# Two fused graph layers, 32 batches of 512 x 512: constant loads as steps, a vector fold in 32-column products, an earlier range check, and new step lists at both ends

## The chip, the cores and the metric

The kernel runs on one core of a Trainium2 chip, in float32 throughout. The metric is the device time of one execution in microseconds. The kernel before was timed three times: median 3287.41 us, from 3285.51 to 3288.52. PE is the engine of matrix products, DVE the vector engine, ACT the scalar engine, POOL the GpSimd engine. SP issues the transfers (DMAs) and computes nothing. Matrix products leave their sums in PSUM banks; all other tiles stand in SBUF.

## What is computed

For each of 32 batches there is a matrix x of 512 nodes by 512 features and a 512 x 512 adjacency, whose rows sum to one. Two layers follow one another:

```python
# layer 0: eight heads of width 64, attention weighted by the adjacency
q, k, v = heads(x @ Wq.T + bq), heads(x @ Wk.T + bk), heads(x @ Wv.T + bv)
logits = q @ k.T / sqrt(64) + log(clip(adj, 1e-8))
x = layer_norm(x + (softmax(logits) @ v) @ Wo.T + bo, gamma, beta)
# layer 1: one head, logits from two vectors, masked by the adjacency
f = x @ fc_w.T + fc_b
logits = (f @ q_w.T + q_b) + (f @ k_w.T + k_b).T + (1 - adj) * -1e9
x = softmax(leaky_relu(logits)) @ f + x
```

The exponential of the logarithm of the adjacency is the adjacency itself, so the kernel multiplies exp(q k) by max(adj, 1e-8) instead of adding a logarithm.

## The kernel before

**Staging.** All work of a batch b is cut into named steps, small functions that each issue a few instructions. A batch has two halves: `first_two` treats head pairs 0 and 1, `second_two` pairs 2 and 3. While batch b is in attention, the halves also carry the output product and layer norm of batch b−1 and layer 1 of batches b−1 and b−2, and the x products of batch b+1. The order of the instructions of PE, DVE, ACT and SP is written by hand: under `manual_schedule` each engine's program has the order in which `perform` calls the steps. There is a list of step names for each half: FIRST and SECOND for batches 2 to 30, and special ones for batch 0 (FIRST0, SECOND0), batch 1 (FIRST1, SECOND1) and batch 31 (FIRST_LAST, SECOND_LAST). Each engine works in order, so a step that waits holds all that stands behind it on its engine, and only on its engine. SP's transfers go round robin over eight semaphores, so that an issue waits until the transfer issued eight before it has landed.

**Steps by name.** S0 to S7 are scores of a head pair (PE, L919, K by Q, 64 rows deep) and their exponentials on ACT (L926 in halves, L928 whole). f.. multiplies by the adjacency (DVE, L934), V.. is the value product (PE, L991, 64 columns for each of two heads), s.. and t.. are sums over the keys (DVE, L946, L950, L957; PE, L1056). The large weight products use Strassen's scheme in Winograd's form: seven products of quarters (`seven`, L226, its matmuls at L221, 64 columns at a time) with additions on DVE and ACT around them. Prefixes name the product: v (values; step m7 of it is vm7, which leaves through the copy L786), p, q and Q (queries and keys of one pair, with the copies L723 and L731 on ACT and additions at L727 on DVE), w (output weights of layer 0), o and O (the last product of layer 1), z (its fc product). d0 to d3 are the differences of x that the v and q products use (DVE, L695). c0 to c3 transpose a quarter of the adjacency each (DVE, L667). g and h are the sums of quarters of the weights wv, wq and wk (DVE, L183, L194). W, O, x, L, H, J, Y, Z steps are the versions for the last batches.

**Head.** Ahead of all steps the load of x of batch 0, the two column blocks `pair`, the weights wv, wq, wk (`load_first_constants`, L159), the adjacency of batch 0 in sixteen pieces (`load_a`, issued at L604) and then the weights wo and fc with bo, gamma, beta and the biases (`load_constants`, L169) are issued on SP. `fold_steps` (L235) issues the loads of fc_b, q_w, k_w, bv and columns of gamma and beta when it is called, also ahead of all steps. X, E and A are the transposes of x of batch 0, their copies, and the first query and key.

**Fold.** Some vectors are folded into others once: bv·Wo into bo (B0, B1), beta·fc into the constant row cc (O0), the products of fc with q_w and k_w (D0 to D7, L265), gamma into fc (G0 to G3, DVE, L306), and the two result vectors spread over all partitions (P0, P1, L284 and L285) as uq and uk. B0 and O0 use `row_times` (L251): four matmuls of 128 x 128 against 128 x 512 in which each column of the vector is broadcast to 128 columns, so that the row that comes out stands in all partitions.

**Range check.** The kernel computes softmaxes without subtracting the maximum, and counts as it goes whether all sums are in range. Steps rg0, rg1, rg2 (`find_range`, L1145 to L1171) reduce these counts to one flag: DVE over the elements, a transpose on PE (`pf`), DVE, a second transpose (`pone`), DVE. In the list they stand at the end. Then every engine loads the flag and branches past a general version of the kernel, which is there for data out of range and does not run here.

**End.** In SECOND_LAST the last product of layer 1 comes in parts (m20, m21 are halves of m2), with additions (a.., b..) on DVE and stores t0 to t4 on SP. `ost0` and `ost1` store the two halves of batch 30's result.

The steps of the last product, among others, have this form:

```python
"rg0": over, "rg1": turn, "rg2": store_flag
...
"m20": lambda: mul(2, "b", ns=(0,)),
"b01": lambda: add_rows(0, 1, "c"), "t2": lambda: store(0, 2, 1),
```

Of the kernel before, what the change touches and what calls it, by code (L numbers as in the profile page):

```python
# [9 lines left out]
FP = mybir.dt.float32  # L10
I32 = mybir.dt.int32
AF = mybir.ActivationFunctionType
# [7 lines left out]
P = 128  # L20
# [5 lines left out]
BL = 32  # L26
# [4 lines left out]
def kernel(  # L31
# [55 lines left out]
    nc = tc.nc  # L87
    B, N, D = x.shape
    DK = D // HEADS
    NC = N // P  # L90
    DC = D // P
# [16 lines left out]
    seen = const.tile([P, 2 * B + 1], FP, name="seen")  # L108
    k_cols = const.tile([P, BL], FP, name="k_cols")
# [4 lines left out]
    def load_weight(w, name, pieces=1):  # L114
        w_sb = const.tile([P, DC, D], FP, name=name)
        load_b(w_sb, w, pieces)
        return w_sb

    def load_row(pool, v, name):
        v_sb = pool.tile([P, v.shape[0]], FP, name=name)  # L120
        nc.sync.dma_start(out=v_sb, in_=v.partition_broadcast(P))
        return v_sb
# [36 lines left out]
    def load_first_constants(pair):  # L159

        for dst, w in zip(pair, (wqT, wkT)):
            nc.sync.dma_start(out=dst, in_=w[:, :P].rearrange("(c p) d -> p c d", p=P))
        K["bq"] = load_col(const, bq, "bq")
        K["bk"] = load_col(const, bk, "bk")
        K["wv"] = load_weight(wvT, "wv")
        K["wq"] = load_weight(wqT, "wq")
        K["wk"] = load_weight(wkT, "wk")

    def load_constants():  # L169
        K["wo"] = load_weight(woT, "wo")  # L170
        K["fc"] = load_weight(fcT, "fc")
        K["bo"] = load_row(const, bo, "bo")
        K["gamma"] = load_row(const, gamma, "gamma")
        K["cc"] = load_row(const, beta, "cc")
        K["q0"] = load_row(const, q_b, "q0")
        K["k0"] = load_row(const, k_b, "k0")
        for name in ("uq", "uk"):
            K[name] = const.tile([P, D], FP, name=name)
        K["qk_s"] = const.tile([P, 3, KH, D], FP, name="qk_s")
        for name in ("v_s", "wo_s", "fc_s"):  # L180
            K[name] = const.tile([P, 3, KH, H], FP, name=name)

# [52 lines left out]
    def fold_steps(banks, psum_parts, scratch):  # L235
# [9 lines left out]
        for row, vec in ((fcb, fc_b), (qw, q_w), (kw, k_w)):  # L245
            nc.sync.dma_start(out=row, in_=vec.partition_broadcast(P))
        with nc.allow_non_contiguous_dma("three vectors"):
            for col, vec in ((bvc, bv), (gc, gamma), (bc, beta)):
                nc.sync.dma_start(out=col, in_=vec.rearrange("(c p) -> p c", p=P))

        def row_times(col, w, bank):  # L251
            for c in range(DC):
                nc.tensor.matmul(
                    bank, col[:, c : c + 1].to_broadcast([P, P]), w[:, c, :],
                    start=(c == 0), stop=(c == DC - 1),
                )
            return bank
# [9 lines left out]
        def constant():  # L267
            cc = K["cc"]
            nc.vector.tensor_add(cc, cc, row_times(bc, K["fc"], banks[1]))
            nc.vector.tensor_add(cc, cc, fcb)  # L270
            nc.vector.tensor_sub(cc[:, H:], cc[:, H:], cc[:, :H])
# [10 lines left out]
        def spread(vector, bank):  # L282
            _, _, _, dg, name, _ = vector
            nc.tensor.matmul(bank, ones, dg, start=True, stop=True)  # L284
            nc.vector.tensor_copy(K[name], bank)  # L285

        def last_parts():
# [9 lines left out]
            "B0": lambda: nc.vector.tensor_add(bo, bo, row_times(bvc, K["wo"], banks[0])),  # L297
# [6 lines left out]
            for i, v in enumerate(vectors) for c in range(DC)  # L304
        } | {
            f"G{c}": lambda c=c: nc.vector.tensor_scalar_mul(  # L306
                fc[:, c, :], fc[:, c, :], gc[:, c : c + 1])
            for c in range(DC)
        }
# [256 lines left out]
    def fast(ctx):  # L566
# [790 lines left out]
        def numbered(steps, prefix):  # L1357
            return {f"{prefix}{i}": step for i, step in enumerate(steps)}
# [134 lines left out]
        def end_steps(b, banks):  # L1493
# [74 lines left out]
            X0 X1 X2 X3 E1 E3 E0 d0 E2 d1 g0 A0 g3 A1 g1 h0 h1 h2 g4 vm1 vcb vm5 vm6  # L1568
            c0 h3 c2 vc12 vm2 d3 vm7 vc22 g2 d2 va22 vc11 c1 vm3 vm4 vc21 h4 va12 S0
            S1 S2 c3 S3 pm1 pcb D0 pm5 pm6 pck2 pm2 pcq2 pcq1 f02 D1 D2 pm4 pm3 pck1  # L1570
            pm7 paq2 pak1 D3 S4 S5 pak2 S6 f12 f10 f03 f01 S7 B0 qm1 qm5 qcb qm6 f00
            qm2 V0a D4 qck2 qcq2 qcq1 ldx f11 qm3 f13 qm7 D5 D6 qaq2 V0b Qm1 D7 V0e
            qak2 qm4 Qcb Qm6 Qm2 B1 s00 qck1 Qm5 s01 Qck2 Qcq2 Qcq1 s02 V1a t00 t01
            V1b s10 V1e s11 Qm7 Qak2 Qm4 Qm3 Qck1 Qak1 Qaq2 s12
        """
        SECOND0 = """
            S0 r0 x0 S1 S2 r3 S3 x1 f22 t10 S4 d0 t11 f21 S5 S6 f20 f23 x3 mv0 S7 x2
            d1 O0 f31 qm1 qm5 V2a dv0 V2b r1 vm1 qck2 qcb qm6 vcb qm2 vm2 d3 s20 f30
            qcq1 V2e qcq2 qm7 G3 G0 qm3 vc11 f32 V3a vm5 f33 d2 s21 s22 V3b vc22
            qak2 vm6 qm4 qaq2 Qm1 qck1 s30 Qcb Qm5 Qck2 vc12 O1 V3e O2 vm3 la Qm6  # L1580
            vm7 s31 s32 Qm2 Qm4 Qm3 c0 Qck1 sc01 va12 r2 va22 Qcq1 Qcq2 t20 vm4 G1
            c1 G2 Qaq2 Qm7 c2 Qak2 Qak1 vc21 c3 sc00
        """
        FIRST1 = """
            t30 S0 S1 t21 t31 S2 S3 f03 f00 f01 S4 S5 S6 f12 mv2 f10 f02 S7 P0 P1
            qm1 qm5 qcb dv2 qck2 qm6 V0a V0b V0e s00 qm2 f11 qm3 qcq1 s01 P2 qcq2
            qm7 f13 qak2 wseed wm1 V1a ldx V1b qaq2 qm4 ldn s02 qck1 wcb V1e fd Qm1
            sc20 sc21 Qm5 fs ws11 t00 s10 wm2 s11 wm6 wm5 ws12 Qck2 wa01 t01 wa11
            Qcb Qm6 wm7 wm3 wa00 wb11 wm4 Qm2 Qm4 s12 wb01 b0 wa10 Qm3 Qcq2 b1 Qcq1
            b2 Qm7 b3 Qck1 Qaq2 Qak1 Qak2  # L1590
        """
        SECOND1 = """
            x0 n0 le1 S0 S1 n2 S2 x2 x1 n4 t10 le0 S3 k1 t11 S4 mv0 S5 mk0 d0 n1 S6
            vm1 k3 n3 x3 S7 k0 qm1 vcb qm5 d1 qcb qck2 R0 k2 u1 k4 d3 kst mk1 f20
            f21 vm5 vm6 vc12 u3 V2a qm6 vc22 u0 f22 f23 u2 qm2 qcq1 qcq2 f30 qm7 u4
            kld f31 f32 V2b dv0 R1 d2 lg0 lg1 f33 V2e vm7 qm3 vm3 lk1 lg2 V3a qak2
            V3b qaq2 lg3 lk2 qm4 lk0 nm lk3 s20 ex2 va12 ex3 Qm1 qck1 R3 vm2 la R2
            ex0 ex1 inv s21 c0 s30 Qcb nr1 nr0 va22 nr3 vc11 s22 V3e Qm5 s31 nr2 Qm6
            Qck2 Qm2 Qcq1 Qm4 Qm3 Qcq2 vm4 t20 s32 c2 Qm7 Qak2 Qck1 sc01 Qak1 c1
            vc21 Qaq2 bl sc00 c3  # L1600
        """
        FIRST_LAST = """
            t21 S0 f00 S1 t30 f01 t31 mv2 S2 S3 y0 S4 f02 e0 S5 S6 e1 zs1 S7 V0a qm1
            qcb qm5 qm6 qm2 qck2 zm1 zcb qm3 y1 f03 qcq2 V0b zA21 zA11 e2 e3 zt1
            zE11 f11 qcq1 zm2 zm5 zm6 zA12 zE12 zc22 zc12 zm3 qaq2 zm7 dv2 Qm1 Qcb
            qm7 fd s00 za12 zE21 s01 za22 qak2 f10 Qm6 zm4 f13 V0e f12 ldn s02 zc21
            t00 Qm2 sc21 qm4 sc20 V1a V1b fs wseed s10 wm1 s11 ws11 s12 zc11 wcb wm5
            wm2 qck1 wa11 Qm5 Qcq2 ws12 wm6 wm3 wa00 wa01 wm7 Qck2 Qm4 wb01 Qcq1 b0
            wb11 wm4 t01 Qm3 b1 Qck1 wa10 Qm7 b2 b3 Qaq2 Qak2 V1e Qak1
        """  # L1610
        SECOND_LAST = """
            t10 n0 zd S0 S1 S2 S3 S4 S5 f20 f23 f21 S6 oseed t11 S7 f22 f31 V2a om1
            n1 zs f30 mv0 ldn H20 n2 V2b n4 k1 n3 k0 k3 k2 os11 H30 u0 ocb om2 k4 u2
            H21 V2e u1 kst f32 om5 om6 os12 u3 le0 u4 V3a dv0 oa00 oa01 H22 f33 om7
            H23 oa11 ob11 H31 kld H32 H24 mk0 V3b V3e H33 Wal sc00 om4 om3 sc01
            Wseed lg1 lk1 yn Wfs lg0 H34 Wm1 Wm5 Wfd lk0 Wcb le1 Ws11 Wa11 mk1 lg3
            lg2 Wm6 Wa01 Wm2 nm ex1 Ws12 lk3 ex0 ex3 Wm7 lk2 Wa00 Wb11 ex2 inv ob01
            nr3 oa10 Wm3 ost1 Wm4 Wb01 b0 nr1 Wa10 nr0 b1 b2 nr2 J0 J1 J2 b3 Lal xn0
            J3 y1 xn1 xk0 xn2 xn3 xle0 xn4 xk1 xk2 ost0 xk3 xk4 xkst Z0 Z1 xu0 y0
            xu2 Yd Z2 xmk0 LN2 xu1 xle1 xkld xmk1 Oseed Z3 Om1 xu3 xu4 Ys xlg1 Os11  # L1620
            xlg0 Ocb xlk1 xlg3 Om5 xlg2 Om6 Oa01 Oa11 Om2 xnm xlk0 Os12 Om7 xlk3
            xex1 xex0 xlk2 Ob11 xex3 xex2 xinv xnr0 Om3 xnr3 Om4 Ob01 LN0 LN1 Lp0
            xnr1 Oa10 Lp1 Ost1 xnr2 Lp2 Oa00 Ost0 Lp3 Le0 Le2 LN3 Le1 Lm1 LT0 Le3
            LT2 LT1 LT3 Lm5 Lcb Ly Lc22 Lm6 Lc12 Lm7 Lm2 La22 Lm4 Lm3 La12 LZ0 Lc11
            LZ1 Lc21 Loseed LZ3 Lom1 Lom4 Locb Lom21 Loa001 Lom20 LZ2 Lom6 Lom5
            Loa10 Loa01 Loa11 Lom7 Loa000 Lot3 Lob10 Lot4 Lob11 Lot0 Lot1 Lom3 Lob01
            rg0 rg1 Lot2 rg2
# [5 lines left out]
        load_a(0, range(NC))  # L1633
        load_constants()
# [9 lines left out]
        head |= fold  # L1644
# [151 lines left out]
```

## Time and profile before

| quantity | value |
|---|---|
| median of three runs | 3287.41 us |
| profiled execution | 3286.61 us |
| its span on the core | 3282.6 us |
| PE busy | 3258.3 us (99%) |
| DVE busy | 3080.4 us (94%) |
| ACT busy | 1471.5 us (45%) |
| POOL busy | 1.0 us |
| mean granted clock of PE | 0.998 |
| HBM read, written | 184.00 MB, 36.72 MB |
| factor products (L934), 512 | 608.7 us, 1210 ns each |
| fold products (L253), 16 records | 592 ns each by the median |

The span is what the profiler sees of the program, the time of the execution is a little longer on both sides. "Busy" is the time in which an engine executes; PE at 99% leaves little idle time for the whole program, and the profile's view of waits lists which engine waited for what, and how long. The chain that ended last follows the work back from the last instruction, and shows which instruction each step had to wait for. A table of stretches gives for each part of the span the busy time of each engine and, as PEclk, the share of PE's full clock that was granted. Batch 2 begins its scores at 198.8 us and batch 31 at 3119.8 us, so a batch takes about 101 us: (3119.8 − 198.8) / 29. The lists that the change lays anew run before the first of these times and after the second.

### The profile page before, as it was taken

To read this page: it belongs to the slowest core of one execution; us is meant where nothing else is said; L and a number is where in the kernel's file an instruction comes from. 1 tells how busy PE (TensorE), PEld (TensorE's weight loads), DVE (VectorE), ACT (ScalarE), POOL (GpSimd) and SP (SyncE) were. 2 spreads that over 40 slices of the span, in tenths; PEclk is the share of its full clock that TensorE was granted. 3 is DMA by queue.
4 is the path that set the end of the run, shared out by engine and by line. 5 is a ranking of instruction groups with operands and counts; after the bars stand their busy time and mean duration, and the time that the engine had idled before them with its cause. 6 is when DMAs were issued, how large, how long until landed. Compare 5 with 4: busy or idle time off the path is not lost.

```text
span 3282.6 us, 64089 instructions
## 1 busy us (share of the span) xinstructions
PE 3258.3 (99%) x25586; PEld 1890.9 (58%) x25586; DVE 3080.4 (94%) x5329; ACT 1471.5 (45%) x2762; POOL 1.0 (0%) x10
## 2 busy tenths in 40 slices
PE   8999999999999999999999999999999999999998
PEld 4555555555655555555555555555555555555655
DVE  6999999999999999999999999999999999999997
ACT  3335534444444454444544444444435534444444
POOL 0000000000000000000000000000000000000000
PEclk9999999999999999999999999999999999999999
DMA  5343433433434434335343344343343443443322
GB/s 129 55 70 71 89 72 66 88 88 72 84 68 74 96 66 91 71 62 95 79 81 82 60 83 93 67 88 68 70 95 70 89 73 67 86 89 71 84 58 67
DMA packets 917263, 256.44 MB, mean 78 GB/s; under 512 B 842720, under 2 KB 844768, under 8 KB 916960
## 3 DMA queue, kind: packets, MB, share of 16 engines
q1 hardware_dynamic: 916960, 252.30, 38.6%
q8 instruction: 203, 3.33, 0.4%
q14 instruction: 100, 0.82, 0.1%
HBM read 184.00 MB, written 36.72 MB: 67 GB/s over the span
## 4 chain that ended last, share of the span: by engine, by line
PE 97%; SPq 1%; ACT 1%; DVE 1%; DMA 0%; issue 0%; DVEq 0%; ACTq 0%
PE f L221 23%; PE my L221 15%; PE mz L221 15%; PE mx L221 15%; PE po L991 13%; PE sc L919 6%; PE mx L919 2%; PE my L919 2%; PE mz L919 2%; SPq L604 0%; SPq L150 0%; PE mx L334 0%; ACT at L926 0%; PE ps L1056 0%; ACT at L928 0%
## 5 line engine op out<-in xcount | busy, mean ns | idle before, releaser
L934 DVE SCALAR_TENSOR_TENSOR at<-cT,at 128x1024 f32<-128x1024 f32 x512 | 608.7, 1210 | 3.3 <-ACT at L928 3.3
L991 PE MATMUL po<-at,v 128*64 128x512 f32 x2048 | 485.1, 595 | 0.1
L723 ACT ACTIVATE qT<-f,bq 128x256 f32<-128x256 f32 x254 | 115.8, 471 | 805.0 <-PE f L221 805.0
L946 DVE TENSOR_TENSOR at<-at,at 128x1024 f32<-128x1024 f32 x378 | 454.5, 1209 | 2.4 <-PE po L991 2.1
L991 PEld LDWEIGHTS po<-at,v 128*64 128x64 f32 x2048 | 141.6, 137 | 223.9 <-issue 131.9
L221 PE MATMUL f<-xT,wq 128*64 128x256 f32 x2032 | 262.7, 379 | 0.5 <-ACT at L928 0.5
L928 ACT ACTIVATE at<-sc 128x1024 f32<-128x1024 f32 x256 | 259.1, 1073 | 5.0 <-DVE ks L957 2.5
L221 PE MATMUL f<-T,qk_s 128*64 128x256 f32 x2032 | 257.0, 379 | 0.4 <-ACT at L928 0.3
L919 PE MATMUL sc<-qT,kT 64*128 64x512 f32 x1024 | 241.9, 589 | 0.0
L221 PEld LDWEIGHTS f<-xT,wq 128*64 128x64 f32 x2032 | 145.5, 137 | 103.0 <-issue 36.3
L221 PEld LDWEIGHTS f<-T,qk_s 128*64 128x64 f32 x2032 | 145.4, 137 | 87.7 <-issue 17.1
L723 ACT ACTIVATE kT<-f,bk 128x256 f32<-128x256 f32 x254 | 120.1, 473 | 136.9 <-PE f L221 128.8
L919 PEld LDWEIGHTS sc<-qT,kT 64*128 64x128 f32 x1024 | 100.4, 187 | 119.6 <-issue 74.9
L950 DVE STREAM_TRANSPOSE at<-at 128x1024 f32<-128x1024 f32 x126 | 154.5, 1226 | 1.1
L957 DVE TENSOR_REDUCE ks<-at 128x32 f32<-128x1024 f32 x126 | 151.5, 1203 | 1.0
L919 PE MATMUL so<-qT,kT 64*128 64x512 f32 x256 | 137.1, 615 | 0.0
L919 PE MATMUL mx<-qT,kT 64*128 64x512 f32 x256 | 132.7, 598 | 1.2 <-ACT v L786 0.7
L919 PE MATMUL mz<-qT,kT 64*128 64x512 f32 x256 | 132.6, 598 | 0.0
L919 PE MATMUL my<-qT,kT 64*128 64x512 f32 x256 | 132.4, 597 | 0.0
L221 PE MATMUL f<-xT,wk 128*64 128x256 f32 x1016 | 131.3, 379 | 1.0 <-ACT qT L723 1.0
L221 PE MATMUL f<-T,wk 128*64 128x256 f32 x1016 | 131.3, 379 | 0.9 <-ACT kT L723 0.9
L221 PE MATMUL f<-xT,qk_s 128*64 128x256 f32 x1016 | 131.2, 379 | 0.0
(383 smaller groups left out, 6380.9 us busy)
## 6 DMA issues: line engine op xcount, KB each, us to landing
cT<-in_adj_dram SPq DMA_DIRECT2D x512, 64.0 KB
R<-d SPq DMA_DIRECT2D x126, 256.0 KB
x<-in_x_dram SPq DMA_DIRECT2D x124, 256.0 KB
L<-in_adj_dram SPq DMA_DIRECT2D x62, 512.0 KB
n<-in_x_dram SPq DMA_DIRECT2D x31, 1024.0 KB
out_dram<-yb SPq DMA_DIRECT2D x62, 512.0 KB
eP<-L SPq DMA_DIRECT2D x480, 64.0 KB
w<-dk SPq DMA_DIRECT2D x32, 256.0 KB
```

The source lines that it names most:

```text
L221: nc.tensor.matmul(to[ts(h, DK)], left[:, ts(h, DK)], right, start=start, stop=stop, skip_group_check=True,)
L723: nc.scalar.activation(of(w, half), ps[bank], AF.Identity, bias=bias)
L919: nc.tensor.matmul(parts[j], s["kT", p][rows, ts(kc, P)], s["qT", p][rows, :], start=True, stop=True,)
L928: nc.scalar.activation(at, sc, AF.Exp, scale=SCALE)
L934: nc.vector.scalar_tensor_tensor(at, cT[:, kc, :].unsqueeze(1).to_broadcast([P, 2, N]), ADJ_MIN, at, ALU.max, ALU.mult,)
L946: nc.vector.tensor_add(to, to, s["at", p, kc])
L950: nc.vector.transpose(flat, flat)
L957: nc.vector.tensor_reduce(ks.rearrange("p h m -> p (h m)"), flat.rearrange("p (a k) -> p a k", k=BL), AX.X, ALU.add,)
L991: nc.tensor.matmul(s["po", p][j * DK : (j + 1) * DK, :], s["v"][h // 4][:, kc, ts(h % 4, DK)], s["at", p, kc][:, j, :], start=(kc == 0), s ...
```

## The change

It has four parts.

1. **Loads as steps.** The loads of wv, wq, wk, wo, fc, the row vectors, the columns and the first adjacency (now in four quarters, la0 to la3, of four pieces each) become steps of the list FIRST0. They stand at the places where the list has them, and SP issues them in that order: wv; quarter 1 of the adjacency; q_w; quarter 2; wk; fc; beta's row; bo; k_w; wo; gamma; wq; bv; quarters 3 and 0; q_b; fc_b; beta's column; k_b; gamma's column; then x of batch 1.
2. **The fold.** `row_times` is replaced by `quarter_rows` and `row_sum`. Each of the four matmuls broadcasts its column of the vector to 32 columns, and writes one quarter of the partitions of a bank, so the four sums stand side by side. ACT copies the bank to SBUF. One further product with `pick`, a column that is 1 at partitions 0, 32, 64 and 96 and else 0, broadcast to 128 columns, adds the four. There are two new steps, Bq and Oq, ahead of B0 and O0. G0 to G3 and the copies of P0 and P1 go from DVE to ACT. POOL gets five small memsets for `pick`.
3. **The range check** goes from the end of SECOND_LAST to places before the last products: rg0 among the O products, rg1 and rg2 among the last products of layer 1, so that pf, pone and the flag stand ahead of Lom3 and Lob11.
4. **The six special lists** are laid anew. In FIRST0, d3 stands ahead of all transposes of the adjacency. In SECOND1, n0 to n3 stand ahead of S0. In SECOND_LAST, the first half of the last product (Lom20), its addition (Loa000) and the stores Lot2 and Lot3 come last, and the store Ost0 of batch 30 after these.

The core of the diff, with the lists cut to the places that are spoken of:

```diff
+    pick = const.tile([P, 1], FP, name="pick")
+    nc.gpsimd.memset(pick, 0.0)
+    for i in range(P // BL):
+        nc.gpsimd.memset(pick[i * BL : i * BL + 1], 1.0)
...
-    def load_weight(w, name, pieces=1):
-        w_sb = const.tile([P, DC, D], FP, name=name)
-        load_b(w_sb, w, pieces)
-        return w_sb
+    def load_weight(w, name):
+        w_sb = K[name] = const.tile([P, DC, D], FP, name=name)
+        return lambda: load_b(w_sb, w)
...
-        def row_times(col, w, bank):
+        def quarter_rows(col, w, bank):
+
             for c in range(DC):
                 nc.tensor.matmul(
-                    bank, col[:, c : c + 1].to_broadcast([P, P]), w[:, c, :],
-                    start=(c == 0), stop=(c == DC - 1),
+                    bank[c * BL : (c + 1) * BL, :], col[:, c : c + 1].to_broadcast([P, BL]),
+                    w[:, c, :], start=True, stop=True,
                 )
+            nc.scalar.copy(more[:, 3, :], bank)
+
+        def row_sum(bank):
+            nc.tensor.matmul(
+                bank, pick.to_broadcast([P, P]), more[:, 3, :], start=True, stop=True)
             return bank
...
-            nc.vector.tensor_copy(K[name], bank)
+            nc.scalar.copy(K[name], bank)
...
-            "B0": lambda: nc.vector.tensor_add(bo, bo, row_times(bvc, K["wo"], banks[0])),
+            "Bq": lambda: quarter_rows(bvc, K["wo"], banks[0]),
+            "Oq": lambda: quarter_rows(bc, fc, banks[1]),
+            "B0": lambda: nc.vector.tensor_add(bo, bo, row_sum(banks[0])),
...
-            f"G{c}": lambda c=c: nc.vector.tensor_scalar_mul(
-                fc[:, c, :], fc[:, c, :], gc[:, c : c + 1])
+            f"G{c}": lambda c=c: nc.scalar.activation(
+                fc[:, c, :], fc[:, c, :], AF.Identity, scale=gc[:, c : c + 1])
...
         FIRST0 = """
-            X0 X1 X2 X3 E1 E3 E0 d0 E2 d1 g0 A0 g3 A1 g1 h0 h1 h2 g4 vm1 vcb vm5 vm6
-            c0 h3 c2 vc12 vm2 d3 vm7 vc22 g2 d2 va22 vc11 c1 vm3 vm4 vc21 h4 va12 S0
-            S1 S2 c3 S3 pm1 pcb D0 pm5 pm6 pck2 pm2 pcq2 pcq1 f02 D1 D2 pm4 pm3 pck1
-            pm7 paq2 pak1 D3 S4 S5 pak2 S6 f12 f10 f03 f01 S7 B0 qm1 qm5 qcb qm6 f00
...
+            X0 lwv X1 X2 la1 X3 E1 lf1 la2 E3 E0 d0 E2 A0 d1 g0 A1 d3 lwk lfc g1 g3
+            lcc vm1 vm5 g2 lbo vcb lf2 h0 lwo vm6 vc12 d2 vm2 lgamma vm7 vc22 g4 vm3
+            vc11 D0 va22 va12 vm4 vc21 h4 S0 S1 lwq S2 S3 lv0 h3 pm1 h1 pcb c2 pm5
+            pm6 pck2 pm2 h2 pm4 D1 pm3 la3 la0 c0 f00 D2 pcq1 pcq2 c3 pck1 paq2 pm7
+            pak1 lq0 S4 c1 S5 pak2 S6 S7 D3 f03 Bq f01 f10 qm1 f02 qcb qm5 V0a lf0
+            V0b qck2 lv2 f11 f13 V0e lk0 f12 qm6 qm2 D4 s00 s01 s02 B0 qcq2 qm3 qcq1
...
         SECOND0 = """
+            S0 S1 S2 t10 t11 x0 x1 x2 S3 d0 x3 d1 S4 f20 S5 f22 S6 S7 Oq qm1 G0 qcb
+            qm5 G2 f30 vm1 f31 mv0 f21 O0 qck2 f23 vcb d3 f33 f32 O1 la V2a dv0 c1
...
         SECOND1 = """
-            x0 n0 le1 S0 S1 n2 S2 x2 x1 n4 t10 le0 S3 k1 t11 S4 mv0 S5 mk0 d0 n1 S6
-            vm1 k3 n3 x3 S7 k0 qm1 vcb qm5 d1 qcb qck2 R0 k2 u1 k4 d3 kst mk1 f20
...
+            n0 t10 n1 n2 n3 S0 le0 k0 x0 t11 n4 x1 f20 S1 S2 S3 x3 le1 k1 x2 S4 S5
+            k2 S6 S7 k3 d0 vm1 mv0 k4 f23 qm1 kst kld qm5 vcb f21 d1 qcb qm6 u0 qck2
...
         SECOND_LAST = """
-            LZ1 Lc21 Loseed LZ3 Lom1 Lom4 Locb Lom21 Loa001 Lom20 LZ2 Lom6 Lom5
-            Loa10 Loa01 Loa11 Lom7 Loa000 Lot3 Lob10 Lot4 Lob11 Lot0 Lot1 Lom3 Lob01
-            rg0 rg1 Lot2 rg2
...
+            Ob01 Lp1 Lp2 rg0 Oa10 Lp3 LN2 LN1 LN3 Le0 Le1 LT0 Le2 Le3 Lm1 LT1 Lcb
+            Lm6 LT2 Lc12 Lm5 LT3 Lc22 Lm7 Lm2 Lc11 La22 Lm4 Ly Lc21 Lm3 La12 Loseed
+            Lom1 LZ0 Locb LZ1 Lom4 Loa10 Lom6 Lom21 LZ2 LZ3 Loa001 rg1 Loa01 Lom5
+            Loa11 Lom7 rg2 Ost1 Lom3 Lob11 Lot4 Lot0 Lob10 Lob01 Lot1 Lom20 Lot2
+            Loa000 Lot3 Ost0
...
         load_first_constants(pair)
-        load_a(0, range(NC))
-        load_constants()
+        loads = constant_steps() | numbered([lambda kc=kc: load_a(0, (kc,)) for kc in range(NC)], "la")
```

## The prediction

> **What bounds the kernel now.** The page of the profile comes first: its span, the busy shares, and the shares of the chain that ended last.
>
> ```profile
> span 3282.6 us, 64089 instructions
> ...
> PE 3258.3 (99%) x25586; PEld 1890.9 (58%) x25586; DVE 3080.4 (94%) x5329; ACT 1471.5 (45%) x2762; POOL 1.0 (0%) x10
> ...
> PE 97%; SPq 1%; ACT 1%; DVE 1%; DMA 0%; issue 0%; DVEq 0%; ACTq 0%
> ```
>
> PE is the bound: 3282.6 − 3258.3 leaves 24.3 us in which it is idle. Batches 2 to 30 keep their order, so the change can win only three things: idle time of PE at both ends, PE work at both ends, and half-speed stretches. The waits of PE say where the idle time is (us in total, times, longest).
>
> ```profile
> PE mx L221 <- DVE xT L695: 3.5, 1, 3.5
> PE my L221 <- ACT at L926: 2.2, 1, 2.2
> PE pf L1162 <- DVE low L1158: 1.9, 1, 1.9
> PE pw_a L221 <- DVE oT L846: 1.2, 1, 1.2
> ```
>
> 3.5 us are in batch 0's V product, 2.2 in SECOND1, 1.9 in the range check, 1.2 in SECOND_LAST. The chain that ended last, in order of time (start, us, what), tells what lies behind the first.
>
> ```profile
> 21.72 2.43 DMA cT<-in_adj_dram
> ...
> 24.28 0.71 DVE cT L667
> 24.99 0.59 DVE xT L695
> 25.58 0.14 issue
> 25.71 3.63 PE mx L221 x16
> 29.34 1.73 PE my L221 x16
> ...
> 48.22 3.63 PE mx L253 x8
> ```
>
> DVE works in order. The last x difference (d3, L695) stands behind the adjacency transposes c0 and c2 (L667), which wait for the transfer of the adjacency. PE stood from 22.18 to 25.71, and vm7 then took 3.63 us where its neighbour of the same size took 1.73. The table of stretches says why (us, PE busy, ..., PEclk, DMA share, GB/s).
>
> ```profile
> 22.00:26.00 4.00, 0.52 (x6) 0.30 (x4) 3.43 (x5) 0.59 (x1) 0.00 (x0) 0.97 0.75 98
> 26.00:29.00 3.00, 3.00 (x16) 2.04 (x14) 0.77 (x2) 0.00 (x0) 0.00 (x0) 0.50 0.77 272
> ...
> 162.00:166.00 4.00, 3.92 (x18) 2.05 (x20) 3.69 (x11) 2.34 (x4) 0.00 (x0) 0.57 0.08 8
> ```
>
> The granted clock was 0.50 after the idle 3.5 us, and 0.57 on average after the idle 2.2 us of SECOND1 (L926 at 162.1). After the 1.2 us at 3207 it stayed full. Both slow stretches lasted 3.41 us, worth 1.7 us of work each.
>
> [...]
>
> **Head: −4.9.** The list FIRST0 now puts d3 ahead of every transpose, behind A1 alone (DVE .59 after 15.1), while vm7 is due at 22.2. The stall of 3.53 goes, and with it 3.63 − 1.73 = 1.9 at half clock: 5.4, so S0 moves from 33.47 to 28.0. What is late next is the transfers, since the steps that issue them (L604 pieces .49 each on SP; a load waits for the eighth before it) now alternate with weights. A megabyte took 2.55 us where wq and wk landed (11.8 to 14.33 for the first). Queue order gives estimates: wk 17.9, fc 20.4, wq 28.1, the last two adjacency quarters (la3, la0) 30 to 32, late case 36. wk is wanted for h0 near 18, wq for h3, and pm1 follows S3 at 32, so both fit. The quarters are wanted by c0 and c3 (.71 each on DVE), ahead of f00, and the query/key additions of pair 1 are queued on DVE behind them; S4 waits for these. S0 to S4 took 44.51 − 33.47 = 11.04; I take 11.6. Then S4 comes at 39.6, a gain of 4.9; bounds 5.5 (nothing late) and 3.6 (quarters at 36).
>
> **Fold: −3.6.** Each `row_times` is 8 records at L253, 3.63 us in the chain (592 ns a record): two are 7.26. In its place come four products of 32 columns and one 128-column product for the sum. The latter has a row: one such product of 512 columns, L284 `my`, took .86. Four of 32 columns side by side have none. Nearest is the value product (L991): 64-column products, two side by side, 8 records in 1.72, .215 a record against .454 at L253. Four side by side would be half of that again, 8 records in .86. One after another: 4 × .86 = 3.45. I take .9 + .9 = 1.8 a set, −1.8 a set, −3.6 in all, because the 64-column row does overlap; the other end is 3.45 + .86 − 3.63 = +.7 a set, +1.4 in all.
>
> [...] The chain above passes from 64-wide products to L253 without any wait (46.50 + 1.72 = 48.22), so by the row a seam costs nothing visible. [...]
>
> The added ACT copies (128x512; L786 takes .59) and G0 to G3 (four of about .7 by ACT's x rows) and the uq/uk copies (.59 each) lie in ACT, which is 45% busy. DVE loses 4 × .46 (L306) and 2 × .68 (L285), 3.2 us: the cover that keeps this stretch on PE, as DVE is busy nearly all the time from 48 on. Should a wait of PE on the copy between quarters and sum appear, it is .6 + about .1, unless qm1's products stand between, as the list has it (Bq well ahead of B0; Oq ahead of O0). POOL's five small memsets run before anything needs them.
>
> **SECOND1: −0.5.** Its list puts n0 to n3 (L398, .70 each on ACT) ahead of S0's exponentials, and the first factors wait for DVE's last additions of the pair before. By rows the exponentials start 2.6 us late, and S4, S5 and vm1 wait some 1.4, .8 and 1.1: 3.3. Before, this list cost 2.2 idle + 1.7 of half clock. Bounds: −3 (the starts overlap) and +1.7 (a slow stretch follows a wait like the 2.2 one). SECOND0 and FIRST1, followed step by step with DVE's start-to-start times (1.2 for 128x1024, .62 for 128x512), leave DVE .5 to .8 us ahead of PE: nothing.
>
> **Tail: −2.2.** The last product ended at 3274.29 and the span at 3282.6, 8.3 later. Between lie:
>
> ```profile
> 3274.32 0.69 DVE qk_s L1327
> ...
> 3276.17 0.28 PE pf L1162
> ...
> 3277.19 0.14 DVE flag L1171
> ```
>
> The flag is done at 3277.33. The trace's own records of uncounted instructions then show .5 us in which every engine loads it, PE's branch for 3.6, and 1.0 to the end: 5.2. Now pf, pone and the flag stand ahead of the last product, so PE goes into load and branch when it ends: 5.2 instead of 8.3, −3.1. PE's two transposes (.27 + .16) move ahead of its end: +.45. SP has Ost0 (512 KB) last, issued some 1.0 after the last product, behind the final add and Lot3; a store of 256 KB took 2.5 us to land (3275.04 to 3277.6), and SP's own load and branch start behind its issue: T + 1.0 + .5 + 3.6 + .7 = T + 5.8. So the end is 5.2 to 5.8 behind; I take +.4, nearer the later. Together −3.1 + .45 + .4 = −2.2; bounds −2.7 (nothing holds it) and −1.5 (a store of twice the row's size lands .7 later still). The cover is that pf and pone find their data ready (rg0 far ahead on DVE); without it PE would wait up to 1.9 inside, and the gain is about nothing.
>
> **End lists: 0.** FIRST_LAST and SECOND_LAST are new throughout. PE's waits in SECOND_LAST were 2.8 us together (1.2 at L846 the longest); they can go (−2.8) or be as large again (+2.8). No row favours either.
>
> **Sum.** −4.9 − 3.6 − .5 − 2.2 = −11.2. The profiled execution took 3286.6 (its span is 3282.6, with 4.0 around it), so 3275.4; the median of the runs shown is 3287.4, .8 above it: 3276.2, given as 3276.
>
> **Rivals.**
> (A) *The 32-column products do not overlap.* +1.4 instead of −3.6: −6.2, 3281. For: no record of this shape exists. Against: the 64-column row. Chance .10.
> (B) *New waits in new lists*: the adjacency quarters at 36 (+1.3), SECOND1 with a slow stretch (+2.2), SECOND_LAST's waits doubled (+2.8). All give −4.9, 3282; one or two −7 to −9, 3279. For: DVE is 94% busy, so any displaced step has no slack. Against: the old lists had 10 us of waits and slow stretches in the same places. Chance .16.
> (C) *The lists close nearly everything*: SECOND1 −3, SECOND_LAST −2.8: −16.5, 3271. Chance .08.
> (D) *Slower: the weights are queued behind adjacency pieces.* For: at 22 to 26 us, with these small pieces under way, DMA moved 98 GB/s, against some 400 GB/s for whole weights. If fc, wo and wq (3.15 MB behind wk) went at 98 GB/s, they would take 32 us, wq would land at 50, and pm1 would start 18 us late with a slow stretch behind: 3276 + 18 + 1.7 = 3296. It decides when wq lands later than 32 + 11 − 1.7 = 41.5, that is below 3.15 MB / 23.6 us = 133 GB/s. Against: in before only adjacency remained to move at 22 to 26, and eight of these loads are held back until wq is issued. Chance .09.
> (E) *The change does less than it says*: the last store or SP's end sets the end in any case and the head's gain is eaten by S4: −3.6 − .5, 3283. Chance .05.
>
> **How the numbers follow.** The forecast (3270 to 3280) has .52. A measurement here tells about 0.2%, 6.6 us, from no change: the edge is 3280.8. Faster: .52 + C .08 + half of A, which sits on that edge, .05 + .09 of B's .16 = .74. Slower: D .09 with .01 of B (a slow stretch in the end lists): .10. Same: the rest, .16. The range runs from 3269 to 3285: A, B, E and most of C lie within, D is left out.
>
> **What would show it.** In the changed profile: no wait of PE on L695 and no 0.50 clock near 26 us; S4 at 39 to 41; a set's quarter products within 1 us (3.4 would be A); the flag ahead of the last product and 5.2 to 5.8 us from that product's end to the span's; PE idle near 15 us in all. Wrong it would be if PE waits at pm1 or h3's users for wq (D), or if DVE is what PE waits for at S4 of batch 0 or S0 of SECOND1 by over 3 us.

## The result and the profile after

| | before | after |
|---|---|---|
| median of 22 runs each | 3285.48 us (3283.85 to 3288.52) | 3281.11 us (3278.06 to 3283.44) |
| profiled execution, span | 3286.61, 3282.6 | 3280.91, 3279.1 |
| from the last product's end to the span's end | 8.29 | 8.37 |
| time outside the span | 4.05 | 1.78 |

The ratio is 0.9985, with an interval from 0.9978 to 0.9991: faster by 4.4 us, clear of noise, but less than half of the 11.2 us that were forecast. The time lies inside the stated range of 3269 to 3285 us and 1.1 us above the narrower forecast of 3270 to 3280. "Outside the span" is the time of the execution less the span that the profiler sees.

The page of the changed kernel, in the lines that answer to those of before:

```profile
span 3279.1 us, 64105 instructions
...
PE 3254.3 (99%) x25590; PEld 1885.3 (57%) x25590; DVE 3077.4 (94%) x5323; ACT 1476.7 (45%) x2770; POOL 1.4 (0%) x15
...
PE 96%; DVE 1%; SPq 1%; ACT 1%; DMA 0%; issue 0%; DVEq 0%
```

PE lost 4.0 us of busy time (3258.3 to 3254.3) and its idle time did not fall: 24.8 us, against 24.3. New waits have taken the place of the old ones, and the view of PE's waits names them.

```profile
PE mz L221 <- DVE L L910: 2.9, 1, 2.9
PE mx L935 <- DVE kT L743: 1.5, 1, 1.5
PE f L221 <- DMA wq<-in_wqT_dram: 1.3, 1, 1.3
PE mz L935 <- ACT at L942: 0.8, 1, 0.8
PE my L221 <- ACT at L942: 0.8, 1, 0.8
```

The waits on L695 and in the range check are gone as forecast. (Longer than these is only the wait for x at the very start, 4.1 us, before 3.7.) The first line is new and the largest; it lies in SECOND_LAST. The next two lie in batch 0, the last two in SECOND1 (before: 2.2 there, in one piece).

To see where time was won and lost, the starts of the scores (K by Q) on PE serve as marks, since both kernels have the same ones:

| mark on PE, us | before | after | difference |
|---|---|---|---|
| S0 of batch 0 | 33.47 | 29.08 | −4.39 |
| S4 of batch 0 | 44.51 | 42.52 | −1.99 |
| S0 in SECOND0 | 70.88 | 67.46 | −3.42 |
| S0 of batch 1 | 112.77 | 107.92 | −4.85 |
| S0 in SECOND1 | 153.63 | 148.58 | −5.05 |
| S0 of batch 2 | 198.83 | 191.43 | −7.40 |
| S0 of batch 31 | 3119.81 | 3111.55 | −8.26 |
| S0 in SECOND_LAST | 3170.31 | 3161.90 | −8.41 |
| end of the last product | 3274.27 | 3270.76 | −3.51 |
| end of the span | 3282.56 | 3279.13 | −3.43 |

Before the last half batch the change is worth 8.4 us. SECOND_LAST gives 4.9 back, and the end gains nothing in the span. The chain of the changed kernel shows how the 4.9 come about:

```profile
3218.53 0.29 SPq L441
3218.82 0.04 issue
3218.87 2.93 DMA out_dram<-yb
...
3221.89 1.22 DVE yb L537
...
3228.88 0.61 DVE L L910
3229.50 0.04 issue
3229.54 3.27 PE mz L221 x16
3232.82 1.75 PE my L221 x16
```

The stretch behind the wait, with its granted clock of 0.59 on average (us, busy time of PE, PEld, DVE, ACT, POOL, then PEclk):

```profile
3229.00:3233.00 4.00, 3.46 (x20) 2.10 (x22) 3.14 (x8) 1.34 (x3) 0.00 (x0) 0.59 0.00 0
```

DVE's multiplication at L537 (step y1) begins batch 30's tile yb, in the place of batch 29's. It waits until batch 29's second store, ost0, has landed. (In SECOND_LAST, ost0 and ost1 store the two halves of batch 29's result and not, as the description of the kernel before has it, of batch 30's; those are Ost0 and Ost1.) On SP this store stands behind xkst, four small transfers of batch 31's k values (L441) that wait for a result of DVE at 3217.5. DVE waited 4.4 us in all, the sum at L910 came late, PE waited 2.88, and its next 16 products took 3.27 instead of 1.75: the granted clock had fallen to 0.50 from 3228.86 on, for 3.41 us.

The end, from the timeline (start, us, engine, line):

```profile
3270.66 2.13 SPq L1346 DMA_DIRECT2D out_dram<-qk_s  x2
3270.81 0.42 DVE L1343 TENSOR_TENSOR qk_s<-mx,qk_s 128x256 f32<-128x256 f32 x1 [0.17 <-PE mx L221]
3272.84 0.45 SPq L890 DMA_DIRECT2D out_dram<-yb  x1
```

The last line is Ost0. Its issue began 2.1 us after the last product, and the last of its bytes landed at 3277.62, 4.8 us after that beginning; SP's final wait for it ended at 3277.63, and the span 1.5 later. PE's own branch ran from 3269.04 to 3273.25; its sequencer took it while products were still queued.

### The profile page after: what moved, and what is told of

It is laid out like the page before. It is cut to its first block, busy times and chain, and to the rows that moved or that the text cites. A ratio compares the mean times of both kernels' runs of the same rounds, so it can differ in the third digit from the quotient of the medians.

```text
span 3279.1 us, 64105 instructions
## 1 busy us (share of the span) xinstructions
PE 3254.3 (99%) x25590; PEld 1885.3 (57%) x25590; DVE 3077.4 (94%) x5323; ACT 1476.7 (45%) x2770; POOL 1.4 (0%) x15
## 4 chain that ended last, share of the span: by engine, by line
PE 96%; DVE 1%; SPq 1%; ACT 1%; DMA 0%; issue 0%; DVEq 0%
PE f L221 23%; PE mz L221 15%; PE my L221 15%; PE mx L221 15%; PE po L1007 14%; PE sc L935 7%; PE mx L935 2%; PE my L935 2%; PE mz L935 2%; SPq L620 1%; DMA fc<-in_fcT_dram 0%; PE ps L1072 0%; DVE n L866 0%; DVE st L382 0%; DVE at L962 0%
```

## The experiments

All times are medians. There are three sets, e1 to e4, e5 to e8 and e9 to e12, each timed on another chip beside its own runs of the kernel before (3285.11, 3285.23 and 3285.34). The marks are those of the table above, from each kernel's one profiled execution.

**e1: ost0 earlier.** The changed kernel with this edit in SECOND_LAST, which moves nothing but one transfer on SP:

```diff
-            oa00 inv nr2 nr0 xle1 ost1 Wb01 nr1 nr3 Wa00 ob01 b0 J0 Wa10 J2 J1 b1
+            oa00 inv nr2 nr0 xle1 ost1 Wb01 nr1 nr3 Wa00 ob01 ost0 b0 J0 Wa10 J2 J1 b1
-            ost0 xu0 xu2 Z2 xu1 xkld Oseed xmk1 Z3 Yd xu3 xu4 LN0 Om1 y0 Ys xlg0 Om5
+            xu0 xu2 Z2 xu1 xkld Oseed xmk1 Z3 Yd xu3 xu4 LN0 Om1 y0 Ys xlg0 Om5
```

> The changed kernel with one step moved: in SECOND_LAST the store ost0 of batch 29 stands behind ob01 instead of behind xkst, which moves one transfer on SP and nothing on the other engines. Theory A (the store stood behind the k transfers of batch 31 on SP, and the next use of the tile yb on DVE waited 4.4 us for it to land): the wait of DVE at L537 goes, the 2.9 us wait of PE on L910 goes, the slow stretch behind it (3.27 us for 16 matmuls that take 1.75 elsewhere) goes; the last product ends 4 to 4.6 us earlier against batch 31's start, and the time falls from 3281.1 to about 3276.7. Theory B (the new list simply has too many DVE steps ahead of Ys): DVE's wait goes, but PE still waits at least 1.5 us on L910, and the time falls by 1 to 2 us.

3277.18 us, 3.9 less than the changed kernel. From S0 in SECOND_LAST to the last product 104.43 us instead of 108.86. Neither L537 nor PE at L910 waits, and the same products run at full clock (e1's PE timeline):

```profile
3226.19 1.95 PE L221 MATMUL my<-fc,L 128*64 128x256 f32 x16
3227.96 1.90 PE L221 MATMUL mz<-fc_s,L 128*64 128x256 f32 x16
3229.69 1.90 PE L221 MATMUL my<-fc_s,L 128*64 128x256 f32 x16
```

A group of products starts every 1.73 to 1.77 us without a gap. The position of one store cost 4.4 us; theory B (too many DVE steps) is out.

**e2: Ost0 earlier.** The changed kernel with:

```diff
-            Loa11 Lom7 rg2 Ost1 Lom3 Lob11 Lot4 Lot0 Lob10 Lob01 Lot1 Lom20 Lot2
-            Loa000 Lot3 Ost0
+            Loa11 Lom7 rg2 Ost1 Ost0 Lom3 Lob11 Lot4 Lot0 Lob10 Lob01 Lot1 Lom20 Lot2
+            Loa000 Lot3
```

> The changed kernel with the store Ost0 of batch 30 moved from the end of SECOND_LAST to directly behind Ost1, on SP alone. Theory A (the 512 KB store, issued 2.1 us after the last product and landed 6.9 us after it, holds the end): from the last product's end to the span's end 5.2 to 5.9 us instead of 8.35, so the span falls by 2.5 to 3.1 and the time by as much. Theory B (the end is set by the branch of PE, 4.2 us long, and the barrier behind it): no change within 0.5 us, because that branch already ran during the last products.

3279.06 us, 2.05 less. From the last product to the span's end 5.38 instead of 8.37: within the 5.2 to 5.9 of theory A. The median fell by less than those 3.0; in the profiled execution S0 of batch 0 came 0.8 later than in the changed kernel's, which this edit cannot cause (see the launches, below).

**e3: both.**

> The changed kernel with both stores moved (ost0 and Ost0). If the two mechanisms are separate, the gains add: 4.4 + 2.8 = 7.2 us, about 3274. If the first only hands its time to another wait in the end list, clearly less than the sum.

3274.69 us: 6.4 less than the changed kernel, against 6.0 for the sum of the two medians and 7.4 for the two terms of the trace. The mechanisms are separate. The ratio to the kernel before is 0.9965 (0.9951 to 0.9978).

**e4: d3 alone.** The kernel before with:

```diff
-            c0 h3 c2 vc12 vm2 d3 vm7 vc22 g2 d2 va22 vc11 c1 vm3 vm4 vc21 h4 va12 S0
+            d3 c0 h3 c2 vc12 vm2 vm7 vc22 g2 d2 va22 vc11 c1 vm3 vm4 vc21 h4 va12 S0
```

> The kernel before with one step moved: in FIRST0 the last x difference d3 stands ahead of the adjacency transposes c0 and c2; loads, fold, range check and all other lists stay. Theory A (the stall of 3.5 us and the slow stretch behind it were only a matter of DVE's order): S0 of batch 0 comes at 28.0 to 28.3 instead of 33.47. What follows tells whether the new order of the loads was needed: if the gain lasts to S4 (39 to 40, from 44.5) the new load order gave 3 us of it away; if S4 stays at 42 or later, the transfers of adjacency (27.5) and of q_w (37.5, which the dot product D0 on DVE waits for) hold it in this order too. In time I expect -3 to -5 us against the kernel before.

3282.75 us, 2.4 less than the kernel before (0.9993, 0.9984 to 1.0002: not clear in the times). That is less than the 3 to 5 us expected. In the trace the stall and the slow stretch are gone. S0 came at 29.88 and not at the expected 28.0 to 28.3: the clock was granted in full 1.15 us later than in the trace of before (9.86 against 8.71), and PE waited 0.8 us for a sum of weights on DVE (L187). What was won at S0 lasts to S4 (e4, PE):

```profile
29.88 0.69 PE L919 MATMUL mx<-qT,kT 64*128 64x512 f32 x1 [0.68 <-ACT v L786]
...
40.94 0.69 PE L919 MATMUL mx<-qT,kT 64*128 64x512 f32 x1 [0.55 <-DVE kT L727]
```

S0 to S4 is 11.06, as before (11.04), where the changed kernel has 13.45. So moving d3 needed no new order of loads, and with the new order S4 follows S0 2.4 us later.

**e5: wo later.** e3 with the step lwo taken from ahead of vm6 and put behind la0.

> e3 with one load moved on SP: the weights wo (1 MB, wanted only by Bq at about 47 us) are issued behind the last adjacency quarters la3 and la0 instead of ahead of wq. Theory A (batch 0 lost its gain at S4 because wq, 33.9, and behind it the key and query additions came late): wq lands 2 to 3 us earlier, PE's 1.3 us wait for it goes, S0 to S4 shrinks from 13.2 to 11.5 to 12, and the time falls by 1 to 1.7 us against e3. Theory B (the bandwidth is not the limit, but the wait for the eighth transfer before): wq lands less than 1 us earlier and S4 stays within 0.5 us.

3272.77 us, 1.9 less than e3. Yet S0 to S4 stayed (13.42 against 13.23), because S0, which no moved transfer feeds, came 1.9 earlier in the profiled execution (28.42 and 30.30; the clock was granted in full at 9.05 and 12.19). wq landed at 33.23, 1.7 earlier than in e3, and S4 came 1.7 earlier with it; PE still waited 1.2 for wq. From wk's landing to wq's took 11.9 us, and 13.1 to 14.6 in the seven traces with the old place of wo, so moving wo did bring wq forward. How much of the 1.9 us it is worth one launch can't tell: with the same order of loads wq landed anywhere from 33.92 to 35.86. What the traces do show is that S4 stands 8.60 to 8.61 us behind wq's landing in all eight that have this order of DVE's steps (the changed kernel, e1 to e3 and e5 to e8; for instance 33.92 and 42.52, 34.93 and 43.53). In the changed kernel DVE goes from wq's landing to the last addition ahead of S4 without a wait.

**e6: range check at the end.** e3 with rg0, rg1 and rg2 taken out of their places and put behind Lot3, the last step.

> e3 with the range check rg0, rg1, rg2 put back to the end of SECOND_LAST, behind the last addition. Theory A (an early flag saves the chain behind the last product and lets PE's branch run under the last products): from the last product to the span's end about 8.3 instead of 5.7, the last product itself .4 earlier since pf and pone no longer stand ahead of it, and the time outside the span back from 1.8 to the 3.7 or so that every run of the kernel before shows, if that gap belongs to the late branch: in all 3.5 to 4.5 us slower than e3. Theory B (the gap outside the span has nothing to do with the branch): it stays 1.8, and e6 is about 2.2 us slower.

3276.33 us, 1.6 more than e3, less than both theories. The last product came 1.03 earlier (103.40 from S0 in SECOND_LAST, e3 104.43), the end 2.69 later behind it (8.42 against 5.73). The early check is worth 1.7 net. The time outside the span stayed at 1.83: theory B on that point.

**e7: full-width fold.** e3 with this in the place of `quarter_rows` and `row_sum`, and Bq and Oq empty:

```diff
+        def row_times(col, w, bank):
             for c in range(DC):
                 nc.tensor.matmul(
-                    bank[c * BL : (c + 1) * BL, :], col[:, c : c + 1].to_broadcast([P, BL]),
-                    w[:, c, :], start=True, stop=True,
+                    bank, col[:, c : c + 1].to_broadcast([P, P]), w[:, c, :],
+                    start=(c == 0), stop=(c == DC - 1),
```

> e3 with the fold's products as in the kernel before: four products of 128 columns for bo and for cc at the places of B0 and O0, no quarter products, no copy, no sum product. The quarter products took .99 and the sum 1.05 in the changed kernel, the full set 3.63 in the kernel before, so I expect 2 x 1.6 = 3.2 us more, all of it on PE: about 3277.9. If the set hides stalls (PE waiting for the exponentials at these places), less: 1.5 to 2.5.

3279.88 us, 5.2 more. From S4 of batch 0 to S0 of batch 1 e7 took 70.14, e3 65.40: 4.7 more, of which 3.2 are the products. Most of the rest are waits that the shorter set does not have (.49 and .8 on the exponentials at L938).

**e8: batch 1's old lists.** e3 with FIRST1 and SECOND1 as they were before.

> e3 with the lists FIRST1 and SECOND1 of the kernel before. From the first score of batch 1 to that of batch 2 the kernel before took 86.1 us and the changed one 83.5. Theory A (the old SECOND1 keeps its wait of 2.2 us on L926 and the slow stretch behind it): 2 to 3.5 us slower than e3, with a granted clock near 0.5 for some 3.4 us. Theory B (the wait came from what SECOND0 left behind, and the new lists ahead of it take it away): within 1 us of e3.

3278.04 us, 3.35 more. S0 in SECOND1 to S0 of batch 2 took 45.22, which is the kernel before (45.20) and not e3 (42.86). Its waits on PE show the old line again:

```profile
PE f L221 <- DMA wq<-in_wqT_dram: 2.3, 1, 2.3
PE my L221 <- ACT at L942: 2.2, 1, 2.2
```

The clock was granted at 0.5 from 159.20 to 162.62, as theory A had it. The wait belongs to this pair of lists. (The first line lies in batch 0, where wq landed at 35.86 in this launch, and a second slow stretch followed it; this profiled execution took 1.8 us longer than e8's median.)

**e9: wq early.** e5 with:

```diff
-            X0 lwv X1 X2 la1 X3 E1 lf1 la2 E3 E0 d0 E2 A0 d1 g0 A1 d3 lwk lfc g1 g3
+            X0 lwv X1 X2 la1 X3 E1 lf1 la2 E3 E0 d0 E2 A0 d1 g0 A1 d3 lwk lwq lfc g1 g3
-            vc11 D0 va22 va12 vm4 vc21 h4 S0 S1 lwq S2 S3 lv0 h3 pm1 h1 pcb c2 pm5
+            vc11 va22 va12 vm4 vc21 h4 S0 S1 S2 S3 lv0 h3 pm1 h1 pcb D0 c2 pm5
```

> e5 with wq issued on SP directly behind wk, ahead of fc, and the dot product D0 (which wants fc) moved on DVE from ahead of va22 to behind h1. In the changed kernel, e3 and e5 S4 of batch 0 came 8.6 us after wq had landed, each time (33.9 and 42.5, 34.9 and 43.5, 33.2 and 41.8). Theory A (wq's landing sets S4 through the DVE steps behind it): wq lands near 24, S0 to S4 falls from 13.2 to 13.4 to about 11.1, which is what the kernel before has, and the time by 2 to 2.4 us against e5 and e3. Theory B (DVE's queue ahead of the key additions is too long whatever wq does): S0 to S4 stays at 12.5 or more. The launch itself varies: the clock went to full between 7.2 and 12.3 us in the runs so far, which moves S0 by up to 1.7 us, so S0 to S4 decides.

3272.08 us, from 3271.77 to 3272.74; ratio to the kernel before 0.9959 (0.9945 to 0.9972). It beats both kernels. wq landed at 22.57. On DVE the step that wants wq (h3, L188) is, in the changed kernel and then in e9:

```profile
33.94 1.22 DVE L188 TENSOR_TENSOR wk<-wq,wk 128x1024 f32<-128x1024 f32 x1 [5.94 <-DMA wq<-in_wqT_dram]
```

```profile
28.52 1.22 DVE L188 TENSOR_TENSOR wk<-wq,wk 128x1024 f32<-128x1024 f32 x1
```

It no longer waits, and S4 follows S0 after 11.04 us (29.67 and 40.71): theory A, to the hundredth what the kernel before needed. The times did not fall by the expected 2 to 2.4 against e5 but by .7. In the profiled pair S0 came 1.25 later than in e5, by the launch, so that S4 came 1.13 earlier and not 2.4; and the span ended 5.77 us behind the last product instead of 5.22, for which no cause was sought.

**e10 and e11: parts that should do nothing.** e10 is the kernel before with only the memsets of pick, e11 with only G and P on ACT.

> The kernel before with nothing but the five small POOL memsets for pick, which is not used. The time outside the span was 3.2 to 4.1 us in all runs of the kernel before and 3.3 to 3.8 with d3 moved, against 1.7 to 2.0 in all kernels built from the changed one, whatever was undone in them (range check, fold products, lists of batch 1, stores). Theory A (the length of the instruction streams decides when the last block of instructions is fetched, and POOL's stream is the one): the gap falls to about 1.8 and the time by 1.9 us. Theory B: gap and time as before.

> The kernel before with G0 to G3 and the copies of P0 and P1 on ACT instead of DVE; nothing else. DVE loses 3.2 us of work in SECOND0 and FIRST1, where PE waits for nothing, so I expect no gain inside the span: within 0.7 us, or up to 2 us worse where ACT's copies delay exponentials. For the time outside the span: 3.7 as before if it does not belong to the streams of ACT and DVE, 1.8 if it does.

3287.35 (ratio 1.0005, 0.9996 to 1.0014) and 3286.78 (1.0003, 0.9994 to 1.0012): no difference that these runs can tell. The time outside the span was 3.71 and 3.78: neither part alone shortens it.

**e12: the fold alone.** The kernel before with pick, quarter_rows and row_sum, and with the places

```diff
-            pm7 paq2 pak1 D3 S4 S5 pak2 S6 f12 f10 f03 f01 S7 B0 qm1 qm5 qcb qm6 f00
+            pm7 paq2 pak1 D3 S4 S5 pak2 S6 f12 f10 f03 f01 S7 Bq qm1 qm5 qcb B0 qm6 f00
-            S0 r0 x0 S1 S2 r3 S3 x1 f22 t10 S4 d0 t11 f21 S5 S6 f20 f23 x3 mv0 S7 x2
-            d1 O0 f31 qm1 qm5 V2a dv0 V2b r1 vm1 qck2 qcb qm6 vcb qm2 vm2 d3 s20 f30
+            S0 r0 x0 S1 S2 r3 S3 x1 f22 t10 S4 d0 t11 f21 S5 S6 f20 f23 x3 mv0 S7 Oq x2
+            d1 f31 qm1 qm5 O0 V2a dv0 V2b r1 vm1 qck2 qcb qm6 vcb qm2 vm2 d3 s20 f30
```

> The kernel before with the new fold alone: pick, quarter products with the copy on ACT at Bq and Oq, the sum product at B0 and O0 some products later; loads, G and P, range check and lists otherwise as before. The quarter products and sum took 2.04 us a set against 3.63. If that is what the fold is worth: 3.2 us less by the first score of batch 1. In e3 the opposite step cost 5.0 us in the median, 4.6 inside the head; the rest beyond 3.2 there were waits that came with it. Theory A: -3.0 to -3.4. Theory B (with the shorter set PE comes to the exponentials too early, and waits instead): -1 to -2.

3285.3 us (0.9996, 0.9987 to 1.0005): no gain. From S4 of batch 0 to S0 of batch 1 it took 67.84, against 68.26 before: .4 us, less than either theory. The products themselves are as short as in the changed kernel (e12, PE):

```profile
50.35 1.06 PE L258 MATMUL mx<-wo,fold_more 128*32 128x512 f32 x8
51.35 1.08 PE L225 MATMUL f<-xT,wq 128*64 128x256 f32 x8
...
53.23 1.12 PE L265 MATMUL mx<-fold_more,pick 128*128 128x512 f32 x2
54.28 1.08 PE L225 MATMUL f<-T,qk_s 128*64 128x256 f32 x8
...
57.31 1.94 PE L1003 MATMUL po<-at,v 128*64 128x512 f32 x8 [1.08 <-DVE at L946]
```

But PE then waits for the factors on DVE (1.08 here) and for exponentials on ACT (.9), 2.0 us in all, in a stretch in which the kernel before has no wait. PE's busy time fell by 2.4 (68.26 to 65.84), and the waits took 2.0 of it back. With e3 and e7 this gives all four pairs of fold and lists, from S4 of batch 0 to S0 of batch 1:

| us | fold of before | new fold |
|---|---|---|
| lists of before | 68.26 | 67.84 (e12) |
| new lists | 70.14 (e7) | 65.40 (e3) |

The fold is worth .4 in the old lists and 4.7 in the new ones, which were laid for it: with the old fold they are 1.9 slower than the old lists. DVE is busy for 62.5 to 62.7 us in all four, so the new lists take no work from it here; it is the order of the steps that lets PE run without a wait. e12 tried one placing of the new steps in the old lists; a better one is not excluded.

In e12's profiled launch the stall on d3 was longer (6.3 us), so its end times say nothing of the fold. In all its eleven runs the time outside the span was 1.8 instead of 3.7, and yet the time did not fall: the median span was 3283.4, against 3281.6. (e10 and e11 have spans of 3283.3 and 3283.0 with the long time outside, so the spans of this set do not tell the fold from the launches.)

## Why the prediction was right, and where it was wrong

| step | forecast | measured in the profiled pair |
|---|---|---|
| head, to S4 of batch 0 | −4.9 | −2.0 |
| fold, S4 of batch 0 to S0 of batch 1 | −3.6 | −2.9 |
| batch 1 and its echo in batch 2 | −0.5 | −3.4 |
| end lists, with .45 for pf and pone | +.45 | +4.75 (FIRST_LAST −.15, SECOND_LAST +4.9) |
| tail, without that .45 | −2.7 | +.1 |
| outside the span | 0 | −2.3 |
| sum | −11.2 | −5.7 |

The two profiled executions differ by 5.7, the medians by 4.4; the profiled execution of before was 1.1 slower than its own median. That the time came to lie in the range is in part luck: the end lists and the tail lost 7.1 us against the forecast, the head 2.9 and the fold .7, while batch 1 gained 2.9 more, and 2.3 came from outside the span, for which the forecast had no term.

**Head: right mechanism, wrong size.** The stall and its slow stretch went, and e4 shows that d3's place alone does it. Of the missing 2.9, 1.1 lie ahead of S0 (29.08, forecast 28.0): the clock was granted in full 1.4 us later in this launch than in that of before (10.09 and 8.71), about .7 of work, and PE waited .4 longer for x. (The .7 is an estimate: the eight 128 x 512 products that began at 8.00 took 4.72 us and the next eight 3.60, so about half of the 2.09 us ahead of the grant was lost.) The other 1.85 lie between S0 and S4, and there the term that was mis-sized is the estimate of wq's landing: 28.1, measured 33.92. Half of the 5.8 us lies ahead of wk, which landed at 20.80 instead of 17.9: wv landed 1.1 later than before, and the eight adjacency pieces and q_w's row behind it, 0.79 MB, took 4.2 us (12.90 to 17.06), 190 GB/s. The other half lies between wk and wq: 4.2 MB (three weights and four broadcast rows of 256 KB) took 13.1 us, 320 GB/s, where the forecast had 2.55 us for each weight of 1.05 MB, 410 GB/s. S4 stands 8.6 behind wq's landing, and in e9 S0 to S4 is back at 11.04 with wq issued earlier. PE did wait for wq at pm1 (1.3 us), one of the signs of being wrong that the prediction names for rival D; but D counted only from a landing at 41.5 on. Rival B had "quarters at 36": the last piece landed at 37.58, and it was wq that decided.

**Fold: right, for a reason that was incomplete.** The four 32-column products run side by side: .99 for the set, where one after another would have been 3.45 by the forecast's estimate (4 × .86). PE shows no wait where the products change their width (at 46.16, 47.15, 54.19 and 55.24), so rival A is out. The sum took 1.05 instead of .9: the forecast's row, .86, was the second of two such products, and the first of them, behind the scores, took 1.06 in before. By these prices the two sets save 3.2. PE has no wait in this stretch in either trace, and yet it became only 2.9 shorter, so other products took .3 longer; whether the added changes of width do that was not tested. And e12 shows that the gain is not the fold's own: it needs lists whose order keeps PE from waiting.

**Batch 1: too cautious.** The forecast's new waits were there in kind (.8 and .8 on L942), but together 1.6 rather than 3.3, and no slow stretch followed. Idle time of PE that before had later on (1.0 us at 170 to 180, .4 at 200 to 220) went as well. e8 puts 3.3 of the 3.4 on this pair of lists.

**End lists: the step that failed.** The prediction said "No row favours either". There was a row, in the view of waits of before:

```profile
DVE yb L521 <- DMA out_dram<-yb: 1.0, 1, 1.0
```

DVE already waited 1.0 us at y1 (L521) for a store of yb, so the stores on SP had no time to spare there, and the new list puts xkst ahead of ost0. The queue of SP was followed through the head and not through SECOND_LAST. The end lists were put at 0, with .45 for pf and pone, and cost 4.75; e1 prices this one store at 4.4. Without it .3 is left, near the .45 that was forecast for pf and pone.

**Tail: right mechanism, wrong cover.** With Ost0 out of the way the end follows the last product after 5.38, 5.73, 5.22, 5.33 and 5.77 us (e2, e3, e5, e7, e9), inside the forecast 5.2 to 5.8; e8 took 6.46, for which no cause was sought. The check ahead of the last product saves 2.69 behind it, but costs 1.03 before it and not .45, so it is worth 1.7 net (e6). But Ost0 was known to be last. The sum let SP branch behind its issue, though SP waits for its landing. Its issue began 1 us later than assumed (Lot2's issue took 1.5), and from there the landing took 4.8 us. The bound of −1.5 was not wide enough.

**Outside the span: not foreseen, and by the count half of what was measured.** All runs of the kernel before took 3.2 to 4.1 us outside the span, the changed kernel 1.8. The medians of the spans differ by 2.2 (3281.4 to 3281.6 against 3279.25), the rest of the 4.4 is this. In the trace the last transfer of an instruction queue ends 4.3 us after the last instruction before, and 1.4 after. Neither d3's place (3.5), the memsets (3.7), G and P on ACT (3.8) nor a late range check (1.8 kept) accounts for it. The fold alone switches it (e12: 1.8), yet without the fold it stays near 2 (e7). Which property of the program decides it is open, and so is whether a shorter time outside makes the execution shorter: in e12 it did not.

## What to carry to other kernels

Walk every queue of a hand-written order to its end, the transfer queue above all: one store behind four small transfers cost more (4.4) than the stretch with the new fold won (2.9), and one weight behind others that nobody needed yet cost half of the head's gain. Where two engines are close to even, a shorter product on one of them can give little until the order of the steps on the others is laid anew for it (here .4 us in the old lists, 4.7 in the new). Before the last instruction, ask what the final wait is for: here the last bytes to land (3277.62), not the last product (3270.76).

## What the runs showed of the hardware

**A slow stretch followed some waits of PE and not others.** A slow stretch, at a granted clock of 0.50, lasted 3.41 us (once, in e12, 6.83). One followed the waits of 3.5 and 2.2 us in before, of 2.3 and 2.2 in e8, of 2.8 in e10 and of 2.9 in the changed kernel. None followed the 2.7 of e7 or the 2.2 of SECOND1 in e4 and e11. So in these traces the length of a wait alone does not tell whether a slow stretch comes behind it.

**Launches differ.** The first grant of full clock came between 7.15 and 12.25 us in the fourteen profiled executions, and S0 of batch 0 at 28.95 to 30.34 for one and the same FIRST0. So a difference of a microsecond between two profiled executions can be the launch's, and the marks were read from one mark to the next. The spread itself differs: e9's five runs lie within 1.0 us, e1's seven within 3.8, the 27 runs of the kernel before beside e9 within 6.8. One likely reason, not tested: the kernel before has waits of 1.8 to 6.3 us at d3 (before, e10 to e12) and of 2.2 us in SECOND1, and behind the latter a slow stretch came in the trace of before and none in those of e4 and e11, while e9 has no wait above .82 behind its launch.

**A 512 KB store at the very end took 4.8 us from the beginning of its issue to its landing** (3272.84 to 3277.62), where 256 KB took 2.6 before (3275.04 to 3277.60), in both cases with other stores still under way. Fifteen of its sixteen parts had landed by 3276.22.
